# A graph layer with gathered senders: rows that SyncE loads come as one tile in each of 26 quads instead of six whole quads, with a third feature buffer and the first group's small steps moved

## The chip, the core and the metric

The kernel runs on one core of one Trainium2 chip. A core has five engines with queues of their own: TensorE (PE: matmuls; PEld is its loading of weights), VectorE (DVE), ScalarE (ACT), GpSimd (POOL) and SyncE (SP), which mainly issues transfers. The metric is the time of one execution in microseconds (us) on the device; lower is better. A comparison uses the median of several executions.

## The reference: what is computed

There are 6250 nodes with 128 features each, and 206250 edges, sorted by receiver. Every edge has two sets of 32 features, a weight, a sender and a receiver. An edge's weights come from two small networks, its score from the receiver's query, the sender's key and those weights, and the senders' values are summed per receiver:

```python
w_ij = jax.nn.silu(edge_feats @ rad_W1 + rad_b1) @ rad_W2 + rad_b2
w_ij = w_ij + (jax.nn.silu(chi_scalar @ sph_W1 + sph_b1) @ sph_W2 + sph_b2)
q_i = (node_feats @ Wq).reshape(-1, NUM_HEADS, HEAD_DIM)[receivers]
k_j = (node_feats @ Wk).reshape(-1, NUM_HEADS, HEAD_DIM)[senders]
alpha = (q_i * w_ij * k_j).sum(axis=-1) / jnp.sqrt(jnp.float32(HEAD_DIM))
alpha = alpha * cutoffs[:, None]
v_j = (node_feats @ Wv)[senders].reshape(-1, NUM_HEADS, HEAD_DIM)
out = jax.ops.segment_sum(alpha[..., None] * v_j, receivers, num_segments=n_nodes) / AVG_NUM_NEIGHBORS
```

There are 8 heads of 16 features; `w_ij` is reshaped to heads too. At the end each node's features plus its sum are normalized to mean 0 and variance 1. Everything is float32.

## The kernel before, in words

**Units.** A tile is 128 edges, one per partition. Four tiles make a quad (`QT = 4`, 512 edges), four quads a group (`NQ = 4`). There are 101 groups and 403 quads; `order` (L131) lists the quads as they are worked, in each group 0, 2, 1, 3. Below, "quad n" is the n-th of this order.

**Node stage.** x is read in 13 chunks. For each chunk PE transposes it (`turn`), multiplies it by the joined weights of K and V (`k_and_v`, L253), DVE copies the result from PSUM (L260), and SP stores it in a table in DRAM, `kv_tab`, one row of 256 floats (1 KB) per node. Beside the chunks run small steps (`beside`, a list by chunk): the receivers' numbers less each quad's first node (`rel`), tables, the first feature load. Then follow the first ten quads (`XQ = 10`) in the same loop: their senders' rows of x were gathered directly by GpSimd (40 gathers, one per tile), and K and V are computed from them, so that they need not wait for the table. After that loop stand small steps: byte offsets of the rows that SP will load (`rows_f`, `at_i`), the sum of the biases as three bf16 rows (`bias_rows`), eleven more turns of `rel` (`turn_rel`, PE and ACT) and their store, and the scaled edge weights (`scale`, L401). The first group's `pick`, `turn_q`, `make_q`, `one_hots_T` and `one_hots` follow at the start of the edge stage.

**Edge stage.** The loop over groups and their four slots (L666 on) writes out one order by hand. For a quad:

- PE: two first layers (`hidden_of`, L446, tile `ph`), the receivers' queries by a one-hot matmul (`q_at_edges`, L457, tile `pq`), the bias (L488) and eight matmuls of the second layers (`weigh`, L493, tile `pw`); the messages of the group before are summed per receiver (L535).
- ACT: the silus (L478) and copies.
- DVE: `multiply` (L501: `pq` by the gathered keys), `scores` (L509, L511, L513), `messages` (L524: the gathered values by the scores).
- GpSimd: the gathers of the senders' rows (`gather`, L125, called by `gathers`, L139), four per quad, each fetching 128 rows of `kv_tab` by indices in `src_i`. They are issued 14 quads ahead (`AHEAD = RING - 2`) into a ring of 16 buffers. In the loop, the gathers of quad n + 14 wait for the last four matmuls of `weigh` of quad n ("no gather ahead of TensorE").
- SP: per group one load of features (`load_feats`, L170, two buffers, two groups ahead), one of receivers' numbers (`load_rel`, L179), one of x (`load_x`, L190), and writes of finished rows (`write_rows`, L624). Feature and x loads also wait for a matmul of the slot.

**Rows by SP.** Six quads (65, 130, 195, 260, 325, 390) are not gathered by GpSimd at all: `load_rows` (L150) has SP read the byte offsets into registers, 16 at a time (L163), and issue one transfer of 1 KB per edge (L167), 512 per quad. It spreads them evenly over the slots up to 8 quads ahead of the use, from slot 0 of the loop. The rows lie in two buffers of a whole quad; the last three quads' wide one-hots (L551) reuse them.

**The end.** The last group has three quads; it is written out behind the loop, with the last quad's multiply and messages in two halves.

Of the kernel before, what the change touches and what calls it, by code (L numbers as in the profile page):

```python
# [47 lines left out]
ROW_QUADS = 6  # L48
ROW_LEAD = 8
ROW_UNIT = 16  # L50
# [8 lines left out]
def gnn_kernel(ctx, tc, x, src, dst, weight, edges, rad_W1, rad_b1, rad_W2, rad_b2,  # L59
# [27 lines left out]
    at_i = const.tile([ROW_QUADS * QT, P], I32, name="at_i")  # L87
# [44 lines left out]
    every = (len(order) - ROW_LEAD) // ROW_QUADS  # L132
    row_at = [(n + 1) * every for n in range(ROW_QUADS)]
    row_quads = {order[i] for i in row_at}
    r_of = {}
# [3 lines left out]
    def gathers(q, marks=()):  # L139

        if q in row_quads:
            return
        kv = quad_of("kv", RING, 2 * D)
        for t in range(QT):
            o = gather(kv[:, t, :], kv_tab, src_i[:, q * QT + t:q * QT + t + 1])
            if marks:
                tc.add_manual_dep(o.ins, marks[t].ins.name, WAIT, reason="no gather ahead of TensorE")
        kv_of[q] = kv

    def load_rows(i):  # L150
# [10 lines left out]
        for u in range(a, min(b, units)):  # L161
            t, e = u * ROW_UNIT // P, u * ROW_UNIT % P
            _, rows = nc.values_load_multi_w_load_instructions(  # L163
                at_i[k * QT + t:k * QT + t + 1, e:e + ROW_UNIT], engines=(SP,), min_val=0,
                max_val=(N - 1) * ROW_BYTES, skip_runtime_bounds_check_because="senders are nodes")
            for p in range(ROW_UNIT):
                nc.sync.dma_start(kv_of[q][e + p:e + p + 1, t, :].bitcast(U8),  # L167
                                  table[:, ds(rows[p], ROW_BYTES)])

    def load_feats(g, mark=None):  # L170
        feats_of[g] = gp.tile([P, EG // 2], F32, name="feats")
        o = nc.sync.dma_start(feats_of[g], edges[g])
        if mark is not None:
            tc.add_manual_dep(o.ins, mark.ins.name, WAIT, reason="one signal of TensorE a quad")
# [4 lines left out]
    def load_rel(g):  # L179

        relb_of[g] = gp.tile([P, EQ], BF16, name="relb")
        r = rel_lin[g * GT:(g + 1) * GT, :].rearrange("(j t) e -> j (t e)", j=NQ)
        nc.sync.dma_start(relb_of[g], r[:, None, :].to_broadcast([NQ, W, EQ]))

# [28 lines left out]
    nc.vector.memset(eps, EPS)  # L213
    nc.vector.memset(ends, 0.0)
    nc.vector.memset(onesb, 1.0)

    with tc.tile_pool(name="nodes", bufs=1) as nodes, \
# [53 lines left out]
        df = nodes.tile([1, NG * NQ], F32, name="df")  # L271
# [8 lines left out]
        def bias_rows():  # L280

            nc.vector.tensor_tensor(b_left, b_in[:, 0, :], b_in[:, 1, :], op=OP.add)
            for i in range(3):
                nc.vector.tensor_copy(b_part, b_left)
                nc.vector.tensor_scalar(b_row[:, i:i + 1], row[:3], float(i), None, op0=OP.is_equal)
                if i == 0:
                    nc.vector.tensor_scalar(b_all, b_part, b_row[:, 0:1], None, op0=OP.mult)
                else:
                    nc.vector.scalar_tensor_tensor(b_all, b_part, b_row[:, i:i + 1], b_all,
                                                   op0=OP.mult, op1=OP.add)  # L290
                if i < 2:
                    nc.vector.tensor_tensor(b_left, b_left, b_part, op=OP.subtract)
            nc.vector.tensor_copy(brow, b_all[:, None, :].to_broadcast([3, QT, D]))

# [51 lines left out]
        def first_rel():  # L346
            turn_rel(0)
            store_rel(0, 1)
            load_rel(0)
# [3 lines left out]
                  7: [first_rel], 10: [lambda: load_feats(0)], 11: [steps]}  # L353
# [14 lines left out]
        for i, (k, n) in enumerate(work):  # L368
# [5 lines left out]
            if i >= len(chunks):  # L374
                kv_of[k[0]] = kvs
                continue
# [11 lines left out]
        rows_f = nodes.tile([P, ROW_QUADS * QT], F32, name="rows_f")  # L388
        for k, i in enumerate(row_at):
            nc.vector.tensor_scalar(rows_f[:, k * QT:(k + 1) * QT],  # L390
                                    src_i[:, order[i] * QT:(order[i] + 1) * QT],
                                    float(ROW_BYTES), None, op0=OP.mult)
        pt = nps.tile([P, QT, P], F32, name="pt", bufs=3)
        nc.tensor.transpose(pt[:ROW_QUADS * QT, 0, :], rows_f, ident)
        nc.vector.tensor_copy(at_i, pt[:ROW_QUADS * QT, 0, :])
# [8 lines left out]
    with tc.tile_pool(name="ps", bufs=1, space=PSUM) as pp:  # L404
        def pick(g):

            n = quads_in(g)
            pick_of[g] = gp.tile([P, NQ, W], F32, name="pick")
            nc.vector.tensor_tensor(
                pick_of[g][:, :n, :], colp[:, None, :W].to_broadcast([P, n, W]),  # L410
                off[:, g, :n, None].to_broadcast([P, n, W]), op=OP.is_equal)

        def turn_q(g):
            n = quads_in(g)
            pt = pp.tile([P, EQ], F32, name="pq", bufs=2)
            o = nc.tensor.matmul(pt[:, :n * W], x_of[g], pick_of[g][:, :n, :], start=True, stop=True)
            for m in made:
                tc.declare_no_dep(o.ins, m.ins, reason="VectorE has read it")
            xT_of[g] = gp.tile([P, P], F32, name="xT")
            return lambda: nc.scalar.activation(xT_of[g][:, :n * W], pt[:, :n * W], AF.Copy)  # L420

        def make_q(g):

            n = quads_in(g) * W
            pt = pp.tile([P, EQ], F32, name="pq", bufs=2)
            nc.tensor.matmul(pt[:n, :D], xT_of[g][:, :n], wq, start=True, stop=True)  # L426
            q_of[g] = gp.tile([P, D], F32, name="q")
            return lambda: nc.scalar.activation(q_of[g][:n, :], pt[:n, :D], AF.Copy)

        def one_hots_T(g):  # L430
            hotT_of[g] = gp.tile([P, EQ], F32, name="hotT")
            nc.vector.tensor_tensor(hotT_of[g], relb_of[g], rowwp.to_broadcast([P, EQ]),  # L432
                                    op=OP.is_equal)

        def one_hots(g):
            hot_of[g] = gp.tile([P, GT, W], F32, name="hot", bufs=3)
            nc.vector.tensor_tensor(  # L437
                hot_of[g], rel[:, g * GT:(g + 1) * GT, None].to_broadcast([P, GT, W]),
                colp[:, None, :W].to_broadcast([P, GT, W]), op=OP.is_equal)

# [7 lines left out]

        made = []
# [48 lines left out]
        def multiply(q, mark=None, t=slice(0, QT)):  # L498
            if t.start == 0:
                kq_of[q] = quad_of("kq", 3)  # L500
            o = nc.vector.tensor_tensor(kq_of[q][:, t, :], pq_of[q][:, t, :], kv_of[q][:, t, :D],  # L501
                                        op=OP.mult)
            if mark is not None:
                after(o, mark)
# [15 lines left out]
        def messages(q, alpha, t=slice(0, QT), marks=()):  # L520

            if t.start == 0:
                msg_of[q] = quad_of("msg", XQ)
            o = nc.vector.tensor_tensor(  # L524
                msg_of[q][:, t, :].rearrange("p t (h e) -> p t h e", e=HD),
                kv_of[q][:, t, D:].rearrange("p t (h e) -> p t h e", e=HD),
                alpha[:, :, :, None].to_broadcast([P, t.stop - t.start, HEADS, HD]), op=OP.mult)
            behind(o, marks, 3)
# [10 lines left out]
        wides = []  # L539

        def wide_one_hots(q):
# [5 lines left out]
            k = order[-3:].index(q)  # L547
            if k % 2 == 0:
                wides.append(quad_of("rows", 2, 2 * D).rearrange("p t (h r) -> p h t r", r=P))
            hot_of[q, "wide"] = wides[-1][:, k % 2]  # L550
# [99 lines left out]
        pick(0)  # L650
        turn_q(0)()
        make_q(0)()
        one_hots_T(0)
        one_hots(0)
        load_feats(1)
        load_rel(1)
        for g in range(1, XL):
            load_x(g)
# [7 lines left out]
        for g in range(NG - 1):  # L666
            for slot, j in enumerate((0, 2, 1, 3)):
# [5 lines left out]
                if slot == 0:  # L673
                    turned = turn_q(g + 1)
                if slot == 1 and 2 <= g:
                    turned = sum_group(g - 2)
                if slot == 2:
                    turned = make_q(g + 1)
# [258 lines left out]
```

## Time and profile before

| | us |
|---|---|
| median of 3 runs | 2011.17 (2010.7 to 2013.14) |
| profiled execution | 2011.89 |
| its span, first to last instruction | 2010.1 |
| PE busy | 1811.3 (90%) |
| VectorE busy | 1466.5 (73%) |
| GpSimd busy | 1505.3 (75%) |
| ScalarE busy | 720.8 (36%) |

The granted TensorE clock is 0.917 of full speed in the mean. The 16 DMA engines are busy about half of the time and move 304.45 MB: 205.62 MB in the queue that GpSimd's gathers use, 95.15 MB in SP's.

How to read it: a group of instructions is named by line, engine, operation and `out<-in`, with its count; then come busy time, mean of one in ns, and the engine's idle time before them with what ended it. The engine that a wait names is the one whose signal came last. POOLq and SPq are the sequencers of those engines: SP's issues of transfers are shown in its queue and are not counted as busy time. The chain of waits is followed back from the last instruction, at each step to what released it; it shares out the whole span.

### The profile page before, as it was taken

The numbers are of one execution on the slowest core, as the hardware profiler recorded it, in microseconds if no ns is written. First come the engines' busy times: TensorE is split into PE (matmuls) and PEld (weight loads), VectorE is DVE, ScalarE is ACT, GpSimd is POOL, SyncE is SP. The second block draws the span as 40 slices with busy tenths as digits, with TensorE's granted clock in tenths as the row PEclk, the third lists the DMA queues.
The fourth block names the chain that finished last, engine by engine and source line by source line (L and its number), as shares of the span: only waits on it lengthen the run. The fifth ranks groups of instructions, "written<-read, shape, count | busy, mean of one in ns | idle before, by whom it ended". The sixth has DMA issues, their size and how long they took to land.

```text
span 2010.1 us, 50508 instructions
## 1 busy us (share of the span) xinstructions
PE 1811.3 (90%) x16012; PEld 1519.6 (76%) x16012; DVE 1466.5 (73%) x3015; ACT 720.8 (36%) x1426; POOL 1505.3 (75%) x1596
## 2 busy tenths in 40 slices
PE   9898988999998988998998999988889889988897
PEld 7787877877877777777777777777777777777786
DVE  6687777878877776766767677767676776767687
ACT  2343333444343333333333332333332333323333
POOL 7777777777777777777777777777777777777775
PEclk9898988999998998998999889889998998898898
DMA  8454555555555555554554545554545555555553
GB/s 312 131 154 139 157 143 150 157 155 153 156 156 149 147 155 147 148 150 144 156 154 139 153 145 150 143 152 142 154 142 152 152 144 154 143 149 144 151 150 89
DMA packets 146414, 304.45 MB, mean 151 GB/s; under 512 B 36717, under 2 KB 79581, under 8 KB 146141
## 3 DMA queue, kind: packets, MB, share of 16 engines
q0 software_dynamic: 75584, 205.62, 36.6%
q1 hardware_dynamic: 69056, 95.15, 14.8%
q8 instruction: 127, 2.08, 0.4%
q14 instruction: 147, 1.20, 0.2%
q10 hardware_dynamic: 1500, 0.40, 0.1%
HBM read 287.58 MB, written 13.46 MB: 150 GB/s over the span
## 4 chain that ended last, share of the span: by engine, by line
PE 53%; DMA 20%; DVE 11%; issue 6%; ACT 4%; POOL 3%; SPq 2%; DVEq 0%; ACTq 0%; POOLq 0%
PE pw L493 27%; DMA kv<-kv_tab,src_i 17%; PE pq L457 10%; PE ph L446 7%; DVE kq L501 4%; PE po L535 4%; PE pw L488 2%; DMA feats<-in_edges 2%; DVE side L511 2%; DVE kq L509 2%; POOL msg L125 2%; POOL kv L125 1%; SPq L167 1%; ACT L478 1%; ACT y L612 1%
## 5 line engine op out<-in xcount | busy, mean ns | idle before, releaser
L125 POOL DMA_INDIRECT kv<-kv_tab,src_i x1548 | 1465.3, 947 | 474.3 <-PE pw L493 186.0
L478 ACT ACTIVATE act<-ph,b 128x512 f32<-128x512 f32 x806 | 518.4, 685 | 1150.5 <-PE pq L457 1124.0
L493 PE MATMUL pw<-w,act 128*128 128x128 f32 x6448 | 915.1, 300 | 0.0
L493 PEld LDWEIGHTS pw<-w,act 128*128 128x128 f32 x6448 | 834.8, 209 | 105.8 <-issue 93.9
L446 PE MATMUL ph<-feats,w 32*128 32x512 f32 x1612 | 497.2, 676 | 41.0 <-ACT act L478 20.9
L457 PE MATMUL pq<-q,hotT 32*128 32x128 f32 x3224 | 495.8, 296 | 42.6 <-DVE kq L501 42.6
L501 DVE TENSOR_TENSOR kq<-pq,kv 128x512 f32<-128x512 f32 x398 | 273.4, 687 | 331.9 <-DMA kv<-kv_tab,src_i 188.2
L457 PEld LDWEIGHTS pq<-q,hotT 32*128 32x128 f32 x3224 | 416.8, 198 | 79.9 <-issue 50.6
L511 DVE TENSOR_REDUCE side<-kq 128x32 f32<-128x512 f32 x404 | 280.2, 693 | 42.7 <-PE pw L493 0.9
L524 DVE TENSOR_TENSOR msg<-kv,side 128x512 f32<-128x512 f32 x398 | 273.2, 686 | 43.2 <-PE pq L457 0.9
L509 DVE TENSOR_TENSOR kq<-pw,kq 128x512 f32<-128x512 f32 x404 | 274.5, 679 | 0.1
L446 PEld LDWEIGHTS ph<-feats,w 32*128 32x128 f32 x1612 | 136.9, 193 | 123.8 <-issue 80.0
L488 PE MATMUL pw<-brow,onesb 3*128 3x512 bf16 x403 | 161.1, 400 | 0.0
L535 PE MATMUL po<-msg,hot 128*32 128x128 f32 x3200 | 155.7, 292 | 0.0
L574 PE MATMUL pq<-part,to 128*128 128x128 f32 x200 | 46.7, 317 | 82.9 <-DVE kq L501 58.4
L513 DVE TENSOR_TENSOR side<-side,scale 128x32 f32<-128x32 f32 x404 | 80.6, 200 | 42.6 <-DVE side L511 0.5
L574 PEld LDWEIGHTS pq<-part,to 128*128 128x128 f32 x200 | 31.9, 201 | 93.6 <-issue 57.4
L535 PEld LDWEIGHTS po<-msg,hot 128*32 128x32 f32 x3200 | 71.5, 111 | 38.9 <-issue 5.6
L432 DVE TENSOR_TENSOR hotT<-relb,side 128x512 f32<-128x512 bf16 x101 | 68.8, 682 | 34.0 <-DMA relb<-rel_lin 34.0
L437 DVE TENSOR_TENSOR hot<-rel,side 128x512 f32<-128x512 f32 x100 | 66.1, 661 | 0.0
L426 PE MATMUL pq<-wq,xT 128*128 128x128 f32 (+1 forms) x202 | 45.1, 308 | 15.2 <-DVE kq L501 14.4
L125 POOL DMA_INDIRECT msg<-in_x,src_x x40 | 39.0, 976 | 13.5 <-issue 11.6
(107 smaller groups left out, 839.3 us busy)
## 6 DMA issues: line engine op xcount, KB each, us to landing
feats<-in_edges SPq DMA_DIRECT2D x101, 512.0 KB
rows<-kv_tab SPq DMA_DIRECT2D x3072, 1.0 KB
kv<-kv_tab,src_i POOLq DMA_INDIRECT x1548
relb<-rel_lin SPq DMA_DIRECT2D x101, 128.0 KB
x<-in_x SPq DMA_DIRECT2D x101, 64.0 KB
out<-y SPq DMA_DIRECT2D x101, 64.0 KB
kv_tab<-kv SPq DMA_DIRECT2D x12, 512.0 KB
act<-in_x SPq DMA_DIRECT2D x12, 256.0 KB
```

Of the source, the lines that this page charges most:

```text
L125: return nc.gpsimd.indirect_dma_start(out=o, out_offset=None, in_=table, in_offset=bass.IndirectOffsetOnAxis(ap=index, axis=0))
L446: return nc.tensor.matmul(act_of[q, i], w1[r0:r0 + R, :], feats_of[g][r0:r0 + R, c0:c0 + EQ], start=True, stop=True)
L457: o = nc.tensor.matmul(pq_of[q][:, t, :], hotT_of[g][b, t * P:(t + 1) * P], q_of[g][b, :], start=True, stop=True)
L478: o = nc.scalar.activation(act, act_of[q, i], AF.Silu, bias=b1[:, i:i + 1])
L488: nc.tensor.matmul(pw, onesb, brow.rearrange("p t d -> p (t d)"), start=True, stop=False)
L493: o = nc.tensor.matmul(pw[:, t, :], act_of[q, i][:, t * P:(t + 1) * P], w2[:, i, :], start=False, stop=(t == QT - 1 and i == 1))
L501: o = nc.vector.tensor_tensor(kq_of[q][:, t, :], pq_of[q][:, t, :], kv_of[q][:, t, :D], op=OP.mult)
L509: nc.vector.tensor_tensor(m, pw_of[q][:, t, :], m, op=OP.mult)
L511: o = nc.vector.tensor_reduce(alpha, m.rearrange("p t (h e) -> p t h e", e=HD), AX.X, OP.add)
L513: o = nc.vector.tensor_tensor(alpha, alpha, scale[:, q * QT + t.start:q * QT + t.stop, None].to_broadcast([P, n, HEADS]), op=OP.mult)
L524: o = nc.vector.tensor_tensor(msg_of[q][:, t, :].rearrange("p t (h e) -> p t h e", e=HD), kv_of[q][:, t, D:].rearrange("p t (h e) -> p t h ...
L535: o = nc.tensor.matmul(po_of[g][j * W:(j + 1) * W, :], hot_of[g][:, j * QT + t, :], msg_of[g * NQ + j][:, t, :], start=(t == 0), stop=(t = ...
```

## The change

- `ROW_QUADS = 6` gives way to `ROW_TILES = 26`: in 26 quads, spread evenly over quads 34 to 392 (`row_at`), GpSimd gathers three tiles and SP loads the fourth, 128 rows. Offsets are read 32 at a time. The first rows are issued in slot 13.
- `multiply` and `messages` work on such a quad in two pieces (`kv_parts`): three tiles from the ring, one from the row buffer.
- The row buffers are three of half the size ("wide"), which the last quads' wide one-hots also use, one each.
- Features have three buffers; they are loaded three groups ahead.
- `pick`, `turn_q`, `make_q`, `one_hots_T` and `one_hots` of the first group, `bias_rows`, the byte offsets and the turns of `rel` move into the loop over the ten gathered quads. The first loads of `relb` and of features move from chunks 7 and 10 behind the last chunk's store.
- A silu of one column at the start makes ScalarE load that table there.
- `df`, a row of 404 numbers, lies in `rel`, which is overwritten after it is read.

```diff
-ROW_QUADS = 6
+ROW_TILES = 26
+ROW_FIRST = 20
+ROW_LAST = 392
 ROW_LEAD = 8
-ROW_UNIT = 16
+ROW_UNIT = 32
...
-    every = (len(order) - ROW_LEAD) // ROW_QUADS
-    row_at = [(n + 1) * every for n in range(ROW_QUADS)]
+    row_at = [ROW_FIRST + (n + 1) * (ROW_LAST - ROW_FIRST) // ROW_TILES for n in range(ROW_TILES)]
...
-        if q in row_quads:
-            return
         kv = quad_of("kv", RING, 2 * D)
-        for t in range(QT):
+        for t in range(QT - 1 if q in row_quads else QT):
...
-        k = max(i + ROW_LEAD - 1, 0) // every
-        if k >= ROW_QUADS:
+        k = next((k for k in range(ROW_TILES) if i <= row_at[k] - ROW_LEAD), None)
+        start = len(order) if k is None else (row_at[k - 1] if k else ROW_FIRST) - ROW_LEAD + 1
+        if i < start:
             return
-        q, start = order[row_at[k]], max(k * every - ROW_LEAD + 1, 0)
-        slots, units = row_at[k] - ROW_LEAD + 1 - start, EQ // ROW_UNIT
+        q = order[row_at[k]]
+        slots, units = row_at[k] - ROW_LEAD + 1 - start, P // ROW_UNIT
...
-            kv_of[q] = quad_of("rows", 2, 2 * D)
+            row_of[q] = quad_of("wide", 3, P)[:, :2, :].rearrange("p t d -> p (t d)")[:, None, :]
...
+    def kv_parts(q, t):
+
+        if q not in row_quads:
+            return [(t, kv_of[q][:, t, :])]
+        return [(slice(0, QT - 1), kv_of[q][:, :QT - 1, :]), (slice(QT - 1, QT), row_of[q])]
...
-        feats_of[g] = gp.tile([P, EG // 2], F32, name="feats")
+        feats_of[g] = gp.tile([P, EG // 2], F32, name="feats", bufs=3)
...
+    lit = const.tile([P, 1], F32, name="lit")
+    nc.scalar.activation(lit, eps, AF.Silu)
...
-        df = nodes.tile([1, NG * NQ], F32, name="df")
+        df = rel[:1, :NG * NQ]
...
+        def row_bytes():
+            for k, i in enumerate(row_at):
+                c = order[i] * QT + QT - 1
+                nc.vector.tensor_scalar(rows_f[:, k:k + 1], src_i[:, c:c + 1],
+                                        float(ROW_BYTES), None, op0=OP.mult)
...
-            load_rel(0)
...
-                  7: [first_rel], 10: [lambda: load_feats(0)], 11: [steps]}
+                  7: [first_rel], 11: [steps]}
...
+        n = len(chunks)
+        beside.update({n + 1: [lambda: pick(0)], n + 2: [lambda: first_q(turn_q), lambda: one_hots_T(0)],
+                       n + 3: [lambda: one_hots(0)], n + 4: [lambda: first_q(make_q)], n + 5: [bias_rows],
+                       n + 6: [row_bytes], n + 7: [turn_rows]})
...
                 kv_of[k[0]] = kvs
+                a = (i - len(chunks)) * 5 // 4
+                for t in range(a * P + P, min(((i - len(chunks) + 1) * 5 // 4 + 1) * P, NT), P):
+                    turn_rel(t)
+                for f in beside.get(i, []):
+                    f()
                 continue
...
             if i == len(chunks) - 1:
+                load_rel(0)
+                load_feats(0)
                 nc.sync.dma_start(scale, weight)
...
-        bias_rows()
-        for t in range(P, NT, P):
-            turn_rel(t)
...
-            o = nc.vector.tensor_tensor(kq_of[q][:, t, :], pq_of[q][:, t, :], kv_of[q][:, t, :D],
-                                        op=OP.mult)
-            if mark is not None:
-                after(o, mark)
+            for u, kv in kv_parts(q, t):
+                o = nc.vector.tensor_tensor(kq_of[q][:, u, :], pq_of[q][:, u, :], kv[:, :, :D],
+                                            op=OP.mult)
+                if mark is not None:
+                    after(o, mark)
...
         load_feats(1)
         load_rel(1)
+        load_feats(2)
...
-                if slot == 2 and g + 2 < NG:
-                    load_feats(g + 2, past)
-                    load_rel(g + 2)
+                if slot == 2:
+                    if g + 3 < NG:
+                        load_feats(g + 3, past)
+                    if g + 2 < NG:
+                        load_rel(g + 2)
```

`messages` is split in the same way as `multiply`.

More of the change, by code (lines that the diff above doesn't have):

```diff
@@ L86, in gnn_kernel @@
     src_x = const.tile([P, math.ceil(XQ / NQ) * GT], I32, name="src_x")
-    at_i = const.tile([ROW_QUADS * QT, P], I32, name="at_i")
+    at_i = const.tile([ROW_TILES, P], I32, name="at_i")
     scale = const.tile([P, NT], F32, name="scale")
@@ L183, in load_rel, with pick, turn_q, make_q @@
         nc.sync.dma_start(relb_of[g], r[:, None, :].to_broadcast([NQ, W, EQ]))
+    made = []
+    def pick(g):
+        n = quads_in(g)
+        pick_of[g] = gp.tile([P, NQ, W], F32, name="pick")
+        nc.vector.tensor_tensor(
+            pick_of[g][:, :n, :], colp[:, None, :W].to_broadcast([P, n, W]),
+            off[:, g, :n, None].to_broadcast([P, n, W]), op=OP.is_equal)
+    def turn_q(g, pt):
+        n = quads_in(g)
+        o = nc.tensor.matmul(pt[:, :n * W], x_of[g], pick_of[g][:, :n, :], start=True, stop=True)
+        for m in made:
+            tc.declare_no_dep(o.ins, m.ins, reason="VectorE has read it")
+        xT_of[g] = gp.tile([P, P], F32, name="xT")
+        return lambda: nc.scalar.activation(xT_of[g][:, :n * W], pt[:, :n * W], AF.Copy)
+    def make_q(g, pt):
+        n = quads_in(g) * W
+        nc.tensor.matmul(pt[:n, :D], xT_of[g][:, :n], wq, start=True, stop=True)
+        q_of[g] = gp.tile([P, D], F32, name="q")
+        return lambda: nc.scalar.activation(q_of[g][:n, :], pt[:n, :D], AF.Copy)
+    def one_hots_T(g):
+        hotT_of[g] = gp.tile([P, EQ], F32, name="hotT")
+        nc.vector.tensor_tensor(hotT_of[g], relb_of[g], rowwp.to_broadcast([P, EQ]),
+                                op=OP.is_equal)
+    def one_hots(g):
+        hot_of[g] = gp.tile([P, GT, W], F32, name="hot", bufs=3)
+        nc.vector.tensor_tensor(
+            hot_of[g], rel[:, g * GT:(g + 1) * GT, None].to_broadcast([P, GT, W]),
+            colp[:, None, :W].to_broadcast([P, GT, W]), op=OP.is_equal)
     def rows_from(table, at):
@@ L293, in bias_rows, with turn_rows @@
             nc.vector.tensor_copy(brow, b_all[:, None, :].to_broadcast([3, QT, D]))
+        rows_f = nodes.tile([P, ROW_TILES], F32, name="rows_f")
+        def row_bytes():
[3 more added lines that the diff above has]
+                                        float(ROW_BYTES), None, op0=OP.mult)
+        def turn_rows():
+            pt = nps.tile([P, QT, P], F32, name="pt", bufs=3)
+            nc.tensor.transpose(pt[:ROW_TILES, 0, :], rows_f, ident)
+            nc.vector.tensor_copy(at_i, pt[:ROW_TILES, 0, :])
         def firsts():
@@ L387, in gnn_kernel @@
             gathers(q)
[L388 to L395, printed above, removed]
         nc.vector.tensor_tensor(bsum, b2[:, 0:1], b2[:, 1:2], op=OP.add)
-        bias_rows()
-        for t in range(P, NT, P):
-            turn_rel(t)
         store_rel(1, math.ceil(NT / P))
@@ L404, in gnn_kernel @@
     with tc.tile_pool(name="ps", bufs=1, space=PSUM) as pp:
[L405 to L439, printed above, removed]
         def hidden_of(q, i):
@@ L447, in hidden_of @@
                                     feats_of[g][r0:r0 + R, c0:c0 + EQ], start=True, stop=True)
-        made = []
         def q_at_edges(q):
@@ L523, in messages @@
                 msg_of[q] = quad_of("msg", XQ)
[L524 to L528, printed above, removed]
+            for u, kv in kv_parts(q, t):
+                n = u.stop - u.start
+                o = nc.vector.tensor_tensor(
+                    msg_of[q][:, u, :].rearrange("p t (h e) -> p t h e", e=HD),
+                    kv[:, :, D:].rearrange("p t (h e) -> p t h e", e=HD),
+                    alpha[:, u.start - t.start:u.stop - t.start, :, None].to_broadcast(
+                        [P, n, HEADS, HD]), op=OP.mult)
+                behind(o, marks, 3)
         def sum_quads(g, t, j=None):
@@ L537, in sum_quads @@
             return o
-        wides = []
         def wide_one_hots(q):
@@ L546, in wide_one_hots @@
             nc.vector.tensor_scalar(d, d, gb[:, q // NQ:q // NQ + 1], None, op0=OP.subtract)
[L547 to L550, printed above, removed]
+            hot_of[q, "wide"] = quad_of("wide", 3, P)
             nc.vector.tensor_tensor(hot_of[q, "wide"], d[:, :, None].to_broadcast([P, QT, P]),
@@ L649, in gnn_kernel @@
         written = []
[L650 to L654, printed above, removed]
         load_feats(1)
         load_rel(1)
+        load_feats(2)
         for g in range(1, XL):
@@ L673, in gnn_kernel @@
                 if slot == 0:
-                    turned = turn_q(g + 1)
+                    turned = turn_q(g + 1, pp.tile([P, EQ], F32, name="pq", bufs=2))
                 if slot == 1 and 2 <= g:
@@ L677, in gnn_kernel @@
                 if slot == 2:
-                    turned = make_q(g + 1)
+                    turned = make_q(g + 1, pp.tile([P, EQ], F32, name="pq", bufs=2))
                 if 1 <= g:
```

12 lines of the change are left out of this document (8 added, 4 removed).

## The prediction

> **What bounds the kernel now.** I read the page's busy times first, then GpSimd's timeline and the windows, then the waits of SyncE's queue, and the chain last.
>
> ```profile
> PE 1811.3 (90%) x16012; PEld 1519.6 (76%) x16012; DVE 1466.5 (73%) x3015; ACT 720.8 (36%) x1426; POOL 1505.3 (75%) x1596
> ...
> L125 POOL DMA_INDIRECT kv<-kv_tab,src_i x1548 | 1465.3, 947 | 474.3 <-PE pw L493 186.0 <-issue 178.3 <-PE pq L457 38.4
> L501 DVE TENSOR_TENSOR kq<-pq,kv 128x512 f32<-128x512 f32 x398 | 273.4, 687 | 331.9 <-DMA kv<-kv_tab,src_i 188.2 <-PE pq L457 102.9 <-PE pw L493 38.2
> ```
>
> PE has the highest share, and POOL seems to idle for a quarter. But POOL's idle time is 474.3 us over 1548 gathers, 0.306 each. POOL's timeline (start, time, in brackets the idle time before) shows whose it is, and the windows how steady (POOL's busy time is the fifth, its gathers in brackets behind it):
>
> ```profile
> 72.62 0.95 POOL L125 DMA_INDIRECT kv<-kv_tab,src_i  x1 [0.30 <-issue]
> 73.88 0.94 POOL L125 DMA_INDIRECT kv<-kv_tab,src_i  x1 [0.30 <-issue]
> 77.60 0.94 POOL L125 DMA_INDIRECT kv<-kv_tab,src_i  x1 [2.78 <-PE pw L493]
> 78.85 0.95 POOL L125 DMA_INDIRECT kv<-kv_tab,src_i  x1 [0.30 <-issue]
> ```
>
> ```profile
> 160.00:260.00 100.00, 88.37 (x843) 75.26 (x842) 74.91 (x151) 34.96 (x70) 75.68 (x80) 0.91 0.53 152
> 760.00:860.00 100.00, 88.47 (x805) 74.01 (x805) 69.83 (x142) 34.52 (x70) 75.61 (x81) 0.91 0.53 152
> 1860.00:1960.00 100.00, 93.34 (x843) 77.23 (x840) 74.58 (x152) 35.76 (x72) 75.74 (x80) 0.93 0.52 150
> ```
>
> Every gather is followed by 0.30 us of nothing, whoever is named: one gather per 1.25 us, 80 or 81 in each 100 us window. The 40 gathers of x and 1548 of kv start at 3.20 and end at 1993.70; 1588 x 1.2506 = 1986.0, so all real stops together are 4.5 us, of which the 2.78 above is the one large one (2.48 beyond the usual gap). **GpSimd's stream of gathers is the bound; from its end 16.4 us remain to the span's end at 2010.1.** Between a quad's last gather and its first multiply (L501) lie 1.9 to 5 us from quad 116 on: PE waits for gathers there.
>
> Earlier PE does not: quad 10's gathers end at 59.14 and its multiply starts at 111.63; at quad 58 it is 302.42 and 339.25. PE is 52, then 37 us behind, and POOL waits for PE only if that reaches its lead of 14 quads (about 70 us). What holds PE back there is SyncE: its waits (total, times, longest), first from 100 to 400 us, then from 1000 to 1300:
>
> ```profile
> SPq L167 <- DMA relb<-rel_lin: 14.0, 13, 1.7
> SPq L624 <- DMA out<-y: 9.5, 3, 5.7
> SPq L172 <- PE pw L493: 2.2, 7, 0.4
> ```
>
> ```profile
> SPq L624 <- ACT y L612: 26.3, 4, 7.6
> SPq L172 <- PE pw L493: 16.6, 12, 3.7
> SPq L167 <- DMA relb<-rel_lin: 12.6, 13, 1.7
> ```
>
> In 300 us SP waits 2.2 us for PE at the feature loads: it issues all the time, and PE runs at SP's pace. Multiplies of quads 14 and 58 start at 129.22 and 339.25, 4.77 us a quad; of quads 66 and 117 at 376.79 and 594.74, 4.27. The chain gives PE 53%, because it follows PE wherever PE came last; it cannot say that a gather 14 quads on is what the end waits for.
>
> **The change, part by part.** The sum is made on the profiled execution, 2011.89 us (span 2010.1 and 1.79 around it), 0.72 above the median 2011.17.
>
> *Fewer gathers.* Six whole quads took 24 gathers from POOL; one tile in each of 26 quads takes 26. POOL issues 1546 for 1548: 2 x 1.25 = **-2.50 us**. That the tiles are spread does not matter to POOL's sum.
>
> *The stop at 74.8.* Gathers of quad 14 wait for the second half of quad 0's weigh matmuls (L493), which start at 74.83. Before them PE lies idle or in small steps from 61.26 (last K and V matmul) to 69.36 (first ph): row numbers, eleven turns of rel paced by ScalarE's copies (3.20), the bias rows on DVE from 63.07 to 66.28, scale (0.98), pick, turn and make q; then a table load (1.28 at 69.76). The change puts all but scale, one turn and one pick beside the gathers of x, which arrive until 55.7. I expect ph at 62 to 64, 5 to 7 us earlier; 2.5 suffice: **-2.48 us**. Against: DVE does some 8 us more among the K and V copies (bias rows 3.2, 26 row numbers at 0.09 to 0.13, one-hots 0.67 and 0.68, pick 0.27), and behind the first transposed one-hot's wait for relb stand those copies, PE's matmuls with three PSUM buffers, then ACT's turns. relb is now issued behind the last kv_tab store (at 42.45 for scale before) and a landing took up to 6.47 on the chain, so up to 49; DVE was busy 11.35 of 20 us from 40 to 60, which hides most. If none were hidden, the stop would stay: 0 to -2.48.
>
> *One gather stretched.* That at 65.72 took 1.60 us beside brow and scale (DVE, 65.87 to 67.20), 0.65 too long. Both ops stay, brow earlier: +0.35 to -0.65, taken 0. The Trainium skill, "SBUF — State Buffer" (SBUF: two separate sides), says that DVE can lock GpSimd out of a shared port until its op ends; by it the 26 row numbers could each stretch a gather, 2.6 us more. The six like them at 61.91 lay beside gathers of 0.95, so the trace gives 0.
>
> *SyncE's rows.* 3328 row DMAs for 3072. A 16-row unit averaged 7.13 us, 1.24 of it the register load, the rest 0.37 a row. A one-word load takes 0.55, so 32 words cost about 0.55 + 31 x 0.045 = 1.95 and a row 0.43, for 0.446. Before, the first row quad put 512 rows in 58 slots, 8.83 a quad, at 4.77; now 128 in 14.3 (372/26), 8.95, from slot 13 to 384: 4.77 + 8.95 x 0.43 - 8.83 x 0.446 = **4.68 us a quad** (4.5 to 4.9, as the other work between rows was 0.76 to 0.93 a quad, and a 32-row burst of 13.7 us delays relb by up to 7 us more). POOL in those slots needs (4 - 26/372) x 1.25 = 4.915. So PE, some 35 us behind at quad 20 (42.5 before, less the earlier start), gains 0.23 a quad and catches up near quad 170: cost **0**. At 4.9 it would be late to the end (below).
>
> *Third feature buffer.* SP has no spare time to use it early; PE's waits for feats are already hidden under POOL's lead: 0. Without that cover it is worth 20.1 us of PE waits (L446). *Split multiplies and messages*: 52 more DVE ops; a 128x256 takes 0.41 where 128x512 takes 0.69, so a split costs about 0.14 and a row quad 0.3; DVE idles 27%: 0. *Wide one-hots in their own buffers, df in rel*: the same ops, and the wait that orders df stands already: 0.
>
> *The tail.* Last multiplies at 1998.06 and 2001.07, though the last gather ended at 1993.70 and 1.95 is the least lag seen; weigh took 3.78 at 1977.20 and 2.05 after. A luckier stretch saves up to 2.4, another slow one adds 2: taken 0.
>
> Sum: 2011.89 - 2.50 - 2.48 = 2006.9 on the profile, **2006.2** against the median.
>
> **Rivals.**
> 1. *The stop stays, or the tail takes it back.* First ph later than 66.8, or the last quads slow: only the 2.50 is left, 2007.2 to 2011. For: DVE's extra work and relb in the x stage; against: 5 to 7 us where 2.5 are needed. 0.20.
> 2. *SyncE becomes the bound: slower.* From what pace? 18 quads without rows end the run, and PE without SP's rows before it did quads 0 to 10 in 3.84 each, so it can recover 18 x 1.16 = 21 us; of a lag of 35 us, 14 must go in 372 quads: the point is 4.915 - 0.04 = 4.88 us a quad. At 4.90, 35 - 6 - 21 = 8 us late, 2014; at 4.95, 27 late, 2033. For: 4.77 was measured at almost the same rows. Against: the register loads halve, and quads 66 to 117 ran at 4.27 with 7.88 rows. 0.08. The Trainium skill, "DMA: Bandwidth & Descriptors" (Rules for kernel authors), would have many small transfers made into one large and calls those under 64 KB mostly overhead, which speaks for this rival; the 0.37 us of SP per 1 KB row agrees.
> 3. *The chain is right and PE's waits are the time:* the 1.8% under feats, 36 us, goes: 1975. Against: POOL's 80 gathers a window, which no feature buffer moves. 0.02.
> 4. *No tile is moved* (2011): the built order has 1546 gathers. Nil.
>
> Forecast 0.70.
>
> **How the numbers follow.** The forecast's own range is 2003.2 (luckier tail 2.4, stretch 0.65) to 2008.5; rival 1 carries it to 2011.2. That holds 0.9 of the cases less the tails of the forecast: 2003.2 to 2011.2 for 8 in 10. Within 0.2% (4.0 us, about what a measurement here can tell from no change) of 2011.17 is 2007.15 to 2015.2. Of the forecast's 0.70 some 0.57 lies below, of rival 1 0.03, and rival 3: faster 0.62; slower 0.07, from rival 2 above 4.90; the same 0.31.
>
> **What would show it.** Right: 1586 gathers at 1.25 us, no gap of 2.78, the last ending near 1988.7, and some 16 us after it; a first ph before 66. Multiplies 1.9 to 5 us behind their gathers from quad 200 at the latest. Wrong: the gap near 74 there; SP without waits and multiplies tens of us late past quad 300 (rival 2); gathers other than 1.25 apart, which would move all of it.

## The result, and the profile after

| | before | after |
|---|---|---|
| median (lowest to highest) | 2010.98 (2009.61 to 2014.02), 17 runs | 2006.77 (2004.72 to 2007.43), 17 runs |
| profiled execution, span | 2011.89, 2010.1 | 2007.43, 2005.3 |
| first ph, first weigh matmul | 69.36, 74.83 | 64.23, 68.69 |
| gathers, end of the last | 1588, 1993.70 | 1586, 1988.18 |
| from there to the end | 16.4 | 17.1 |

The ratio is 0.9978, 95% interval 0.997 to 0.9985: 4.2 us less (3.0 to 6.0), and 2006.77 where 2006.2 was forecast. Times are in us.

The page of the changed kernel, PE's to POOL's busy times and two groups:

```profile
PE 1806.6 (90%) x16012; PEld 1521.8 (76%) x16012; DVE 1468.5 (73%) x3087; ACT 718.5 (36%) x1426; POOL 1502.9 (75%) x1594
...
L127 POOL DMA_INDIRECT kv<-kv_tab,src_i x1546 | 1463.0, 946 | 471.3 <-PE pw L517 182.9
...
L218 DVE TENSOR_TENSOR hotT<-relb,side 128x512 f32<-128x512 bf16 x101 | 68.9, 682 | 88.7 <-DMA relb<-rel_lin 88.7
```

There are two gathers fewer, each still followed by 0.305 of idle time (471.3 over 1546). VectorE's wait for relb, the receivers' numbers from which it makes hotT (L218), has grown: 34.0 before, 88.7 here and 47.3 in a second profile of this kernel. POOL's timeline where the stop was (start, time, idle time before):

```profile
72.48 0.94 POOL L127 DMA_INDIRECT kv<-kv_tab,src_i  x1 [0.30 <-DMA kv<-kv_tab,src_i]
73.73 0.95 POOL L127 DMA_INDIRECT kv<-kv_tab,src_i  x1 [0.30 <-DMA kv<-kv_tab,src_i]
74.98 0.95 POOL L127 DMA_INDIRECT kv<-kv_tab,src_i  x1 [0.30 <-issue]
76.23 0.95 POOL L127 DMA_INDIRECT kv<-kv_tab,src_i  x1 [0.30 <-issue]
77.48 0.95 POOL L127 DMA_INDIRECT kv<-kv_tab,src_i  x1 [0.30 <-issue]
```

The 2.78 is gone, because the first weigh now starts at 68.69. The windows (POOL's busy time is the fifth, its gathers in brackets):

```profile
160.00:260.00 100.00, 90.57 (x855) 77.01 (x848) 76.48 (x160) 37.62 (x74) 75.56 (x80) 0.90 0.52 148
760.00:860.00 100.00, 90.57 (x808) 76.08 (x810) 74.11 (x154) 34.70 (x70) 75.70 (x80) 0.90 0.53 154
1860.00:1960.00 100.00, 89.13 (x797) 73.91 (x798) 72.82 (x153) 35.30 (x71) 75.62 (x81) 0.93 0.50 146
```

80 or 81 gathers in 100 us, as before. So the last gather ends 5.5 earlier: 2.50 for two gathers, 2.48 for the stop, the rest from 0.0003 less in the mean period (1.2506 and 1.2503), which differs as much between profiles of one kernel (1.2511 in the second). The end gives 0.7 of it back.

SP's waits from 1000 to 1300 (total, times, longest), with the wait at the feature loads fourth:

```profile
SPq L647 <- DMA out<-y: 19.0, 5, 4.9
SPq L647 <- ACT y L635: 14.6, 2, 9.7
SPq L237 <- PE pw L517: 1.7, 5, 0.4
SPq L178 <- PE pw L517: 1.5, 5, 0.4
```

Before, SP waited 16.6 for PE at the feature loads in this stretch; now 1.9 (1.5 and 0.4). SP has hardly anything to spare for PE here. Over the whole run these waits were 77.7 before and are 50.4 (58.3 in the second profile).

### The profile page after: what moved, and what is told of

Its sections match the earlier page's. It is cut to its first block, busy times and chain, and to the rows that moved or that the text cites. A ratio compares the mean times of both kernels' runs of the same rounds, so it can differ in the third digit from the quotient of the medians.

```text
span 2005.3 us, 51075 instructions
## 1 busy us (share of the span) xinstructions
PE 1806.6 (90%) x16012; PEld 1521.8 (76%) x16012; DVE 1468.5 (73%) x3087; ACT 718.5 (36%) x1426; POOL 1502.9 (75%) x1594
## 4 chain that ended last, share of the span: by engine, by line
PE 61%; DMA 16%; DVE 9%; issue 5%; ACT 4%; POOL 3%; SPq 1%; DVEq 0%; POOLq 0%; ACTq 0%
PE pw L517 31%; DMA kv<-kv_tab,src_i 12%; PE pq L481 11%; PE ph L472 8%; PE po L563 4%; DVE kq L526 3%; DMA relb<-rel_lin 3%; PE pw L512 3%; POOL msg L127 2%; DVE kq L534 2%; ACT L502 2%; ACT y L635 1%; DVE side L536 1%; PE pq L212 1%; POOL kv L127 1%
## 5 line engine op out<-in xcount | busy, mean ns | idle before, releaser
L127 POOL DMA_INDIRECT kv<-kv_tab,src_i x1546 | 1463.0, 946 | 471.3 <-PE pw L517 182.9
L481 PE MATMUL pq<-q,hotT 32*128 32x128 f32 x3224 | 505.5, 300 | 65.9 <-DVE hotT L218 43.0
L472 PE MATMUL ph<-feats,w 32*128 32x512 f32 x1612 | 502.3, 680 | 19.8 <-ACT act L502 19.0
L481 PEld LDWEIGHTS pq<-q,hotT 32*128 32x128 f32 x3224 | 424.8, 201 | 95.3 <-issue 57.7
L526 DVE TENSOR_TENSOR kq<-pq,kv 128x512 f32<-128x512 f32 (+1 forms) x404 | 273.8, 678 | 276.6 <-DMA kv<-kv_tab,src_i 122.2
L551 DVE TENSOR_TENSOR msg<-kv,side 128x512 f32<-128x512 f32 (+1 forms) x404 | 273.9, 678 | 42.9 <-DVE side L538 0.5
L218 DVE TENSOR_TENSOR hotT<-relb,side 128x512 f32<-128x512 bf16 x101 | 68.9, 682 | 88.7 <-DMA relb<-rel_lin 88.7
L212 PE MATMUL pq<-wq,xT 128*128 128x128 f32 x200 | 45.9, 316 | 18.6 <-DVE kq L526 18.5
L212 PEld LDWEIGHTS pq<-wq,xT 128*128 128x128 f32 x200 | 35.5, 222 | 21.8 <-DVE kq L526 21.4
```

The costliest lines, as they stand in the source:

```text
L127: return nc.gpsimd.indirect_dma_start(out=o, out_offset=None, in_=table, in_offset=bass.IndirectOffsetOnAxis(ap=index, axis=0))
L472: return nc.tensor.matmul(act_of[q, i], w1[r0:r0 + R, :], feats_of[g][r0:r0 + R, c0:c0 + EQ], start=True, stop=True)
L481: o = nc.tensor.matmul(pq_of[q][:, t, :], hotT_of[g][b, t * P:(t + 1) * P], q_of[g][b, :], start=True, stop=True)
L526: o = nc.vector.tensor_tensor(kq_of[q][:, u, :], pq_of[q][:, u, :], kv[:, :, :D], op=OP.mult)
L551: o = nc.vector.tensor_tensor(msg_of[q][:, u, :].rearrange("p t (h e) -> p t h e", e=HD), kv[:, :, D:].rearrange("p t (h e) -> p t h e", e ...
```

## The experiments

Every ratio is to the kernel before on the same chip. **The first four fell on a chip on which the kernel before takes 2629.56** (2622.16 to 2639.94, 29 runs), with a granted clock of 0.81 to 0.82 in place of 0.92; the later ones on chips with 2010.96 to 2012.94.

| kernel | here | 2011-us chips | ratio there, interval |
|---|---|---|---|
| changed kernel | | 2006.40 | 0.9978, 0.9969 to 0.9987 |
| early steps alone | 2622.77 (0.9970) | 2007.18 | 0.9981, 0.9972 to 0.9990 |
| 26 tiles alone | 2630.57 (0.9998) | 2010.61 | 1.0000, 0.9991 to 1.0009 |
| two feature buffers | 2624.13 (0.9973) | 2009.19 of 2012.94 | 0.9981, 0.9973 to 0.9990 |
| 13 tiles | 2597.49 (0.9859) | 2022.62 | 1.0058, 1.0044 to 1.0072 |
| 28 tiles | | 2042.83 | 1.0160, 1.0141 to 1.0180 |
| 32 tiles | | 2210.26 | 1.0983, 1.0961 to 1.1004 |
| 28 tiles, relb on ScalarE | | 2390.12 of 2012.94 | 1.1867, 1.1839 to 1.1896 |

("here": the 2630-us chip.)

### Four kernels on the 2630-us chip

Early steps alone (the changed kernel with the rows and features as before):

```diff
-ROW_TILES = 26
-ROW_FIRST = 20
-ROW_LAST = 392
+ROW_QUADS = 6
...
-ROW_UNIT = 32
+ROW_UNIT = 16
...
-        feats_of[g] = gp.tile([P, EG // 2], F32, name="feats", bufs=3)
+        feats_of[g] = gp.tile([P, EG // 2], F32, name="feats")
```

> Only the early steps of the change, on the kernel before: six whole row quads, 16 offsets a load, two feature buffers. Gather-stream theory (the time is GpSimd's gathers at 1.25 us each, its stops, and the tail): 1588 gathers as before, the 2.78 us gap near 74 gone, the last gather ending near 1991.2, and 2.5 us less than before: about 2008.5, ratio 0.9988. Rival (PE's waits are the time, and the change wins by the feature and row loads): PE only starts earlier, and loses it to SyncE's feature loads within ten quads: no change, 2011.

26 tiles alone (the kernel before with `row_at`, `load_rows`, `kv_parts` and the row buffers of the change):

```diff
-ROW_QUADS = 6
+ROW_TILES = 26
+ROW_FIRST = 20
+ROW_LAST = 392
...
-ROW_UNIT = 16
+ROW_UNIT = 32
```

> Only the row tiles of the change, on the kernel before: one tile in each of 26 quads, 32 offsets a load, but the small steps behind the gathered x and two feature buffers. Gather-stream theory: 1546 gathers, the gap near 74 stays (2.5 to 3 us), and 2.5 us less than before: about 2008.5, ratio 0.9988. Rival (PE's waits): more rows on a SyncE that already holds PE back, and no third feature buffer: slower than before, by 5 us or more.

Two feature buffers (loads two groups ahead again):

```diff
-        feats_of[g] = gp.tile([P, EG // 2], F32, name="feats", bufs=3)
+        feats_of[g] = gp.tile([P, EG // 2], F32, name="feats")
...
-        load_feats(2)
...
-                if slot == 2:
-                    if g + 3 < NG:
-                        load_feats(g + 3, past)
-                    if g + 2 < NG:
-                        load_rel(g + 2)
+                if slot == 2 and g + 2 < NG:
+                    load_feats(g + 2, past)
+                    load_rel(g + 2)
```

> The changed kernel with two feature buffers again, loaded two groups ahead. Gather-stream theory: PE waits for features again, some 20 us in total while it is behind the gathers, and the time stays: 2006.8 within 1.5 us, ratio 0.998 to before. Rival (PE's waits): the 20 us come back, about 2027.

13 tiles:

```diff
-ROW_TILES = 26
+ROW_TILES = 13
```

> The changed kernel with SyncE loading one tile in 13 quads instead of 26: half of the row transfers, 13 more gathers. Gather-stream theory: 1599 gathers of 1.25 us, 13 x 1.25 = 16.3 us more than the changed kernel: about 2023, ratio 1.006 to before, although SyncE and PE wait less. Rival (SyncE's rows hold PE back and so the time): SyncE is relieved of 1664 rows of 0.43 us, DVE's 89 us of waits for relb go: faster than the changed kernel.

None of the absolute times came, and 13 tiles came out faster, not slower: there the gather stream is not the bound. Busy times, the chain and the gathers of the kernel with two feature buffers:

```profile
PE 2146.5 (82%) x16012; PEld 1782.7 (68%) x16012; DVE 1474.0 (56%) x3087; ACT 725.5 (28%) x1426; POOL 1499.7 (57%) x1594
...
PE 72%; issue 14%; DVE 6%; another core or an unknown queue 5%; ACT 3%; DMA 0%; DVEq 0%; ACTq 0%; SPq 0%
...
L127 POOL DMA_INDIRECT kv<-kv_tab,src_i x1546 | 1460.8, 945 | 1033.2 <-PE pw L517 426.2
```

A gather takes the same 0.945, but POOL idles 1033.2 in place of 471.3: it stops for 1.2 to 2.3 at most quads, at PE's weigh. The same 16012 matmuls take PE 2146.5 in place of 1806.6, and weigh follows weigh every 6.19 in the mean, where the gathers need 4.91. So these four cannot test the theory of the gather stream. With the early steps, PE's first weigh starts at 120.09 (alone) and 121.54 (with 26 tiles and two feature buffers), without them at 125.42 (26 tiles alone). The two kernels that have them gain 6.8 and 5.4 us (0.9957 to 0.9983, and 0.9957 to 0.9989), and the tiles alone nothing that shows (0.9983 to 1.0013). That fits PE as the bound: an earlier start counts there, and tiles moved from POOL do not. The changed kernel itself, with three feature buffers, did not run on this chip.

Why 13 tiles with three feature buffers are 27 us better there than 26 with two stays open. SP waits 556 for PE at the feature loads with 13 tiles and 92 with 26, so SP has little to spare even at 6.2 a quad, and its row issues come unevenly (a quarter over 0.7 apart, where the other chips show 0.32). That SP's delays reach PE is only argued. What makes this chip slower is open too. From 0.816 to 0.907 in granted clock is 11%, less than the 19% that PE's busy time differs by. The lower clock may in part follow from PE's idle time: with two feature buffers it is 0.50 from 20 to 40 us, where PE is busy for 4.97, and on the 2011-us chips it falls to 0.866 with 32 tiles, where PE waits. Some stops have no cause in the profile at all: in the same profile VectorE stands still for 21.0 up to 46.63, and nothing is shown that it waits for.

### The changed kernel and 32 tiles

```diff
-ROW_TILES = 26
+ROW_TILES = 32
```

> The changed kernel itself, to have it on the chip that also runs the kernel with 32 row tiles. Gather-stream theory: GpSimd starts a gather every 1.25 us without a stop from 3.2 us on, so 1586 gathers end at 1988 us and the ratio to the kernel before is 0.998 (2006 us), if the chip grants TensorE a mean clock near 0.91 as in the first profile. Rival, TensorE is the bound where its clock is granted lower (0.81 to 0.82, as in the four runs before, where the kernel before took 2630 us): GpSimd then stops at most quads for 1.3 to 2.2 us because the ring of gathered tiles is full, the weigh group's period is 6.2 us a quad, and the ratio is 0.997, the same as with two feature buffers (0.9973) and as with the early steps alone (0.997), since tiles moved to SyncE take nothing off TensorE.

> 32 tiles on SyncE in place of 26: 768 more row transfers, 6 fewer gathers. Theory in which SyncE is just behind GpSimd at 26 tiles (4.6 us a quad against 4.9): a tile of 128 rows costs SyncE some 55 us (128 times 0.37 us and four register loads of 2 us), so 32 tiles make 11.0 rows a quad and about 5.5 us a quad, past GpSimd's 3.914 gathers x 1.25 = 4.89; on a chip with TensorE's clock near 0.91 the time is then 2180 to 2260 us, 9 to 13% slower, the GpSimd stream stops at most quads, and TensorE waits for x and relb. If SyncE's cost a row were hidden (another bound), six fewer gathers would give 7.5 us less than with 26: 1999 us. On a chip with the clock near 0.81, where TensorE's 6.2 us a quad is the bound, 5.5 us a quad on SyncE still fits: within 0.3% of the kernel with 26 tiles by that theory. If instead the row transfers themselves slow TensorE there (13 tiles gave 0.986, 26 gave 0.997), 32 tiles are slower again by half of that step: 1.002 of the kernel before.

The first is as expected. The second came at 2210.26, within the 2180 to 2260 of the theory that SyncE is just behind GpSimd. Its windows and its waits for relb:

```profile
760.00:860.00 100.00, 81.82 (x678) 69.52 (x679) 64.92 (x138) 30.75 (x61) 69.56 (x75) 0.81 0.47 138
1860.00:1960.00 100.00, 85.34 (x773) 71.74 (x772) 68.16 (x142) 32.79 (x66) 68.42 (x73) 0.88 0.46 136
...
DVE hotT L218 <- DMA relb<-rel_lin: 455.7, 56, 14.8
```

There are 75 and 73 gathers in a window: POOL is held, its ring being full with PE up to 80 us behind the gathers. Multiplies of quads 60 to 360 come 5.42 apart (expected 5.5). What PE misses most is hotT (295.0), which VectorE makes from relb, and SP issues relb behind its rows.

### Both halves again, 13 tiles, and 28 tiles

The first three edits are those above; the fourth is:

```diff
-ROW_TILES = 26
+ROW_TILES = 28
```

> The early steps alone, now on whichever chip is given. It keeps six whole quads on SyncE, so 1588 gathers. Gather-stream theory, where the kernel before takes 2011 us: the stop of 2.78 us at 74.8 us goes, nothing else: last gather begins near 1990.3 us, and the time falls by 2.5 us, to 2008.5 (ratio 0.9988). Rival, in which the earlier start of TensorE itself counts: the first multiply comes 6 to 7 us earlier, and the time falls by as much, to 2004.5. Where TensorE is the bound (the kernel before at 2630 us): 0.997 again.

> The 26 tiles alone. Gather-stream theory, where the kernel before takes 2011 us: 1586 gathers, and the stop near 74.8 us stays at 2.5 to 2.8 us, so the time falls by 2.5 us, to 2008.5 (ratio 0.9988), and the two halves add up to the whole change (0.9978). If the third feature buffer or the early steps were needed for SyncE to keep pace, it is slower than that: SyncE's lead is shorter by some 6 us, which TensorE's catching up at 0.3 us a quad takes back within 20 quads, so I expect nothing of it. Where TensorE is the bound: 1.000 again.

> 13 tiles on SyncE in place of 26: 13 gathers more, 1664 row transfers fewer. Gather-stream theory, where the kernel before takes 2011 us: 13 x 1.25 us = 16.3 us more than with 26 tiles, 2022.7 us (ratio 1.006), with GpSimd without a stop, and SyncE, at 4.6 - 13 x 128 / 372 x 0.42 = 2.7 us a quad of work, waiting for marks of TensorE for a third of the time. If SyncE's transfers were what holds TensorE, it is not slower than with 26 tiles: 2006 or less. Where TensorE is the bound: 0.986 again.

> 28 tiles: 2 gathers fewer than with 26, 256 row transfers more. If GpSimd's stream were the only bound, 2 x 1.25 = 2.5 us less, 2003.9 us. By the rival of the prediction (SyncE is the bound from 4.88 us a quad): between the measured 4.605 us a quad at 26 tiles (8.95 rows a quad) and 5.43 at 32 tiles (11.01 rows a quad) a row costs 0.40 us, so 28 tiles (9.63 rows) give 4.88 us a quad against GpSimd's 3.925 gathers x 1.250 = 4.907. TensorE, some 50 us behind the gathers at quad 10, then comes nearer by 0.03 us a quad, 10 us in all, and is still 35 to 40 us behind at the end: 2030 to 2045 us, with GpSimd stopped now and then by the full ring. Where TensorE is the bound: 0.997 to 1.000.

*Early steps alone*: 2007.18, 3.9 us less, where 2.5 were expected; the interval is 2.0 to 5.6 us. POOL has no stop at the first gather of quad 14:

```profile
74.73 0.95 POOL L125 DMA_INDIRECT kv<-kv_tab,src_i  x1 [0.30 <-PE pw L511]
```

Its 1588 gathers end at 1990.16, 3.5 earlier. PE starts ph 6.6 earlier; if that itself were the gain, the time would have fallen by as much, which lies outside the interval.

*26 tiles alone*: expected 2.5 us less, measured 0.4, with an interval from 1.8 less to 1.8 more. That is a miss, and POOL's timeline shows a cause for part of it:

```profile
73.45 0.95 POOL L127 DMA_INDIRECT kv<-kv_tab,src_i  x1 [0.30 <-issue]
78.42 0.95 POOL L127 DMA_INDIRECT kv<-kv_tab,src_i  x1 [4.02 <-PE pw L499]
```

The stop has grown from 2.78 to 4.02: POOL came to it 0.43 earlier than in the profile before, and left it 0.82 later. DVE shows why it left later; the line of this kernel, and of the changed one:

```profile
61.58 1.66 DVE L397 TENSOR_SCALAR rows_f<-src_i 128x1 f32<-128x1 int32 x26
```

```profile
55.32 1.65 DVE L344 TENSOR_SCALAR rows_f<-src_i 128x1 f32<-128x1 int32 x26
```

The 26 row numbers take 1.66, where six instructions took 0.52 before. Here they stand on the path to the first weigh (75.64 after 74.83), and that costs 0.82 of the 2.50 that two fewer gathers save. In the changed kernel they lie at 55.32, among the K and V copies, well ahead of its first weigh. In this profile the last gather still ends 2.2 earlier than before (1991.47). So the trace gives the tiles a gain of some 2 us, and the medians cannot tell it from nothing.

*13 tiles*: 2022.62 for 2022.7 expected. 13 gathers cost 16.2 us on the median. POOL's group and SP's waits from 1000 to 1300:

```profile
L127 POOL DMA_INDIRECT kv<-kv_tab,src_i x1559 | 1475.3, 946 | 475.1 <-issue 186.5
...
SPq L178 <- PE pq L481: 43.4, 6, 12.7
SPq L237 <- PE pq L481: 41.8, 9, 7.6
```

SP now waits for PE for a third of the stretch, PE is at the gathers' heels from quad 58 on (2.2 behind), and no wait for relb is left. Yet the kernel is slower, by the price of its 13 gathers.

*28 tiles*: 2042.83, within 2030 to 2045. A window, and waits of VectorE over the whole run:

```profile
1860.00:1960.00 100.00, 85.40 (x780) 71.82 (x780) 69.81 (x144) 33.47 (x67) 75.62 (x81) 0.89 0.51 149
...
DVE hotT L218 <- DMA relb<-rel_lin: 288.5, 47, 12.9
```

POOL goes on without a stop and ends at 1984.30, 3.9 earlier than with 26. But 57.8 us remain from there, not 17: multiplies of quads 20 to 380 come 4.92 apart, the gathers 4.91, so PE, 40 us late at quad 20, is 45 late at quad 380. The expected reasons came less well than the number: PE was to come 10 us nearer and the full ring to stop POOL now and then, and neither happened. Between 26 and 28 tiles the bound passes from POOL to SP.

### Two feature buffers again, and relb from ScalarE's queue

The second kernel has 28 tiles and this edit:

```diff
-        nc.sync.dma_start(relb_of[g], r[:, None, :].to_broadcast([NQ, W, EQ]))
+        nc.scalar.dma_start(relb_of[g], r[:, None, :].to_broadcast([NQ, W, EQ]))
```

> The changed kernel with two feature buffers instead of three. Prediction: the third buffer is worth nothing, because TensorE's waits for features come while it is some 40 us behind the gathers or right behind them, and GpSimd's stream ends when it ends: the same as the changed kernel, 2006.4 to 2007 us (ratio 0.998), last gather at 1987 to 1988 us, with TensorE's waits for features back at 10 to 36 us. Rival: the third buffer is what lets SyncE put its row transfers beside the wait for TensorE's mark; without it SyncE loses up to the 20 us of feature waits that the kernel before shows, TensorE catches up later or not, and the time is up to 20 us more, with a longer tail after the last gather.

> 28 tiles, and the 101 loads of relb issued from ScalarE's queue instead of SyncE's. With 28 tiles and all on SyncE the time was 2042.8 us, with VectorE waiting 288.5 us for relb and TensorE about 45 us behind the gathers to the end. A relb load takes SyncE 0.57 us and about 0.1 us around it, 0.17 us a quad, so SyncE's pace falls from 4.88 to 4.71 us a quad against GpSimd's 4.907; TensorE gains 0.19 us a quad, more than 50 us in all, and is at the gathers' heels before the end: 1584 gathers, 2003.9 us (ratio 0.9965), tail 15 to 17 us, VectorE's wait for relb under 30 us. If the row tiles or features are late as well as relb, the time stays above 2020. If issuing on ScalarE, 0.6 us every four quads, delayed the activations that TensorE waits for, it would be behind by up to 60 us: 2040 or more, with waits of TensorE for act grown from 51 us.

*Two buffers*: ratio 0.9981 against 0.9978 with three, intervals nearly the same. The last gather ends at 1990.65, later than the expected 1987 to 1988, as a gather takes 0.948 on this chip, where the kernel before takes 2012.94. PE's waits for features are back (22.0, 7 times) and cost nothing that can be measured.

*relb on ScalarE*, meant as a version that beats both: 2390.12, the worst of all. Of the three expected cases the first is refuted. The other two have no upper bound and cover the number, but not the cause: relb is no longer late, and PE's waits for act have not grown. SP's waits, PE's, and one relb load on ScalarE's queue:

```profile
SPq L167 <- DMA relb<-rel_lin: 474.7, 87, 10.5
...
PE pq L203 <- DMA x<-in_x: 327.2, 57, 10.7
PE ph L472 <- DMA feats<-in_edges: 151.5, 43, 8.5
...
1009.30 0.52 ACTq L189 DMA_DIRECT2D relb<-rel_lin  x1
```

SP's row transfers wait 474.7 us for relb, mostly once per load: around the load above, no transfer of SP starts between 1008.57 and 1013.85. The trace shows what ties the two queues. The 4036 transfers of SP and ScalarE signal eight counters, 504 or 505 each, taken in turn by both queues, and nearly all rows (3537 of 3584) first wait on the counter that they will signal, that is, for the transfer that had it before. At each of these waits that transfer is a load of relb on ScalarE's queue. With relb on SP such a wait lasts 1.8 at most in the kernel before. With relb on ScalarE, a row of SP waits until ScalarE, working through its own activations, has come to the load, and the load has landed. No further run took this apart. DVE no longer waits for relb; now x and the features, behind the rows, are late.

## Why the prediction was right, point by point

- **The bound.** Right. From 13 tiles to 26, the time follows the count of gathers at 1.25 each (16.2 for 13). PE's chain share and its waits, for relb or features, did not decide: with 13 tiles they go and the kernel is slower.
- **Fewer gathers, -2.50.** The count came (1546), and so did the price of a gather, by the 13 above. Two gathers alone do not stand out from the noise of the medians: 0.4 for the tiles alone (1.8 less to 1.8 more), and 0.6 between the early steps alone and the whole change, with intervals that overlap. The traces have the last gather end 2.2 earlier with the tiles alone, 3.5 with the early steps alone, and 5.5 and 4.8 with both.
- **The stop, -2.48.** Right: it is gone with the early steps, and stays without. By the medians the early steps gave 3.9 (2.0 to 5.6), so the sum of 4.2 is better shown than its two equal halves. First ph was forecast at 62 to 64 and came at 64.23 and 61.88 in two profiles. The 26 row numbers, put at 0.09 to 0.13 each, came every 0.06.
- **The stretched gather, 0.** Right: 1.66 for 1.60, again beside `scale`. The Trainium skill, "SBUF — State Buffer" (SBUF: two separate sides), says that certain DVE ops can lock GpSimd out of a shared port. By it the 26 row numbers could have cost 2.6; the gathers beside them took 0.95, as the trace of before had it for six.
- **SyncE's rows, 4.68 a quad.** About right: quads 20 to 117 came 4.605 apart. The earlier start was put at 7 us less lag at quad 20 and gave 2 (40.3 for 42.5; 37.8 in the second profile): PE waited 1.3 for x before 73.81, and quad 10 was as late as before (51.6 and 52.5). PE had caught up by quad 116 in one profile and by quad 170 in the other, forecast near 170. The 1.9 to 5 us that the prediction reads behind quad 116 reach 8.8 in the trace of before (quad 131), and 7.8 after quad 200 in the changed kernel. The margin was as thin as the rival had it: two more tiles turn it.
- **Third buffer and tail, 0.** Right: 0.9981 and 0.9978; and 17.1 and 15.4 for 16.4 in two profiles of the changed kernel.
- **Rival 2** had the right place (4.88 a quad) and too low a price. It gave PE 1.16 a quad back over the last 18 quads, from the 3.84 of quads 0 to 10. At 4.92 its two prices (8 us late at 4.90, 27 at 4.95) give some 16; with 28 tiles 41 came (57.8 less the usual 16.4). Some 5 of that is the lag at quad 20, 40 in place of 35. The rest is the recovery of 21 us, which did not come: quads 387 to 402 came 4.50 apart, and quad 387 came 17.1 after quad 386, as VectorE waited 12.6 for relb, so the lag at the last quad was 46. The Trainium skill, "DMA: Bandwidth & Descriptors" (Rules for kernel authors), which would have many small transfers made one, spoke for this rival. The trace bears it out as a cost of the issuing queue: rows come 0.323 apart, with 2.1 of register load per 32, so 128 of them take SP some 49 us.

## What to carry to other kernels

When a steady stream of issues on one engine is the bound, count its instructions and its stops: the busy share of other engines, and their waits, say nothing while that engine's lead covers them. Before moving work off it, price the queue that takes the work per stage, and the lag that must be made up; here the whole change with 26 tiles gained 0.2%, most of it by the early steps as far as the medians tell, and with 28 tiles it lost 1.6%. A transfer put on another engine's queue can tie the two queues together through the counters they share.

## What the runs showed of the hardware that was not expected

Chips differ: the same kernel took 2010.96 to 2012.94 on some and 2629.56 on another. With two feature buffers on both kinds, a gather took 0.948 and 0.945, but PE's busy time was 1805.3 and 2146.5, 19% longer. There the gathers were not the bound, and the 0.3% that two kernels gained fits PE's earlier start instead. The order of the kernels is not the same either: 13 tiles are the slower version at 2011 us and the faster one at 2630.
